# A fused convolution network on one core: spreading the steps of a group-norm statistic over the chunks of layer 1 and computing its shift there

## The chip, the cores and the metric

The kernel runs on 1 core of one Trainium2 chip. The metric is the device time of one execution in microseconds, the median of several runs. Before the change it is 4012.31 us (three runs, 4012.15 to 4015.99).

## The reference

Four layers work on `x` of shape (2, 128, 64, 64), float32. Each normalizes its input in 32 groups of channels, applies its function and adds the result to `x`:

```python
def _gn(v, G=32, eps=1e-5):
    B_, C_, H_, W_ = v.shape
    g = v.reshape(B_, G, C_ // G, H_, W_)
    m = jnp.mean(g, axis=(2, 3, 4), keepdims=True)
    s = jnp.var(g, axis=(2, 3, 4), keepdims=True)
    return ((g - m) / jnp.sqrt(s + eps)).reshape(v.shape)
...
x = x + _L0_conv_ref(_gn(x), ...)
x = x + _L1_conv_ref(_gn(x), ...)
x = x + _L2_conv_ref(_gn(x), ...)
x = x + _L3_conv_ref(_gn(x), ...)
```

Layers 0 and 3 are attention over the 4096 pixels. Layer 1 sums a depthwise 5x5 convolution with dilation 2, a depthwise 1x5 convolution of a 1x3 convolution, and a product with weights that are themselves a correlation of the input. Layer 2 is a product of quaternions in the frequency domain: a 2-D Fourier transform, a product with stored weights at each frequency, and the transform back. The change lies where layer 1 ends and layer 2 begins.

## The kernel before

The activations `X` stay in on-chip memory as a tile of 128 channels by 2 images by 4096 pixels; each layer adds to it in place. A chunk is 512 pixels, so an image has 8 chunks.

**Order.** Layers 1 and 2 open with `_in_order` (L536, L807; the context manager is at L1328): every instruction of TensorE, VectorE, ScalarE and GpSimd is tied to the one before it on its engine as the program writes them. So the order of each of those queues is the order of the Python code, and nothing moves ahead of a waiting instruction of its queue[...]. DMAs are issued from SyncE's queue.

**The statistics.** `_stats_steps` (L1407) is a generator of 11 steps for one image: eight `bn_stats`, one a chunk (L1418); the aggregation `bn_aggr` (L1421); the mean's step, which is a matmul that averages over each group of four channels (L1424), a copy of the mean to the first column of its result (L1429), a difference (L1431) and a square (L1433); and the variance's step, which is a second such matmul (L1436), the addition of epsilon on VectorE (L1403) and the power -0.5 on GpSimd (L1404), both into the second column. So the result is the mean and the reciprocal deviation of each channel. The caller advances it by `next`, and by that decides between which other instructions a step stands.

**The last loop of layer 1** runs over the images `b` and the chunks `c` (L747 to L768). In chunk 0 and 2 of an image, TensorE first computes eight of the 25 + 5 taps of the depthwise convolutions for half an image as small matmuls (`on_tiles`, L681), and ScalarE copies the sums to a tile `z` (L691). In every chunk it computes seven matmuls into one PSUM bank (`combined`, L710). VectorE then adds to `X` the bank of the chunk before (`added`, L721), and after chunks 1, 3 also the half image `z`. After that VectorE works off some of the taps of the depthwise convolution of the second image (`taps`, L662, each over half an image of 2048 pixels: 4, 2, 4, 2, 3, 2, 2, 2 of them in the eight chunks), and then the loop advances the statistics by two steps. There are no statistics to advance for the first image. When it is finished, its remaining additions are made, and `steps` becomes the generator for the first image as layer 2 needs it (into `there`, a slice of the tile `st` of the kernel's main function). So its steps fall into the second image's chunks: two `bn_stats` in each of chunks 0 to 3, the aggregation and the mean's step in chunk 4, the variance's step in chunk 5, and none is left for chunks 6 and 7. After the loop, the last chunk of the second image is added (L721 again).

**The first loop of layer 2** (from L849) runs over the images. VectorE first computes `shift`, minus the mean times the reciprocal deviation (L852). ScalarE normalizes eight columns of the image at a time (`normalized`, L860), and two steps of the second image's statistics follow in VectorE's queue; TensorE transposes them (L870), VectorE copies the result (L876), TensorE multiplies by the Fourier matrix (L883), ScalarE copies the product to `y` (L884). This is skewed over eight such blocks an image. Ahead of it stand three small memsets (L810, L816, L817) and SyncE's loads of the first spectral weights (L823).

The tile `st` in the main function has a slice of two columns for each of the two images of layer 1, for the first image of layer 2 and for that of layer 3.

Of the kernel before, what the change touches and what calls it, by code (L numbers as in the profile page):

```python
# [10 lines left out]
F32 = mybir.dt.float32  # L11
AF = mybir.ActivationFunctionType
ALU = mybir.AluOpType
# [3 lines left out]
B, C, H, W = 2, 128, 64, 64  # L17
# [514 lines left out]
def _layer1(ctx, tc, X, a, cst, here=None, there=None, consts=None):  # L532


    nc = tc.nc
# [183 lines left out]
    def added(b, lo, x):  # L719
        to = X[:, b, lo : lo + x.free_size()]  # L720
        nc.vector.tensor_add(to, x, to)  # L721

    def some(gen, n):
        for _ in range(n):
            next(gen, None)
# [21 lines left out]
    steps = iter(())  # L747
    ready = []
    for b in range(B):
        for c in range(NCH):  # L750
            if c in (0, 2):
                z = on_tiles(g[b], t2[b], c // 2)
            ps = combined(t9[b], t2[b], c)

            for x in ready:
                added(*x)
            ready = [(b, c * CH, ps)]
            if c in (1, 3):
                ready.append((b, c // 2 * S // 2, z))
            some(rest, (4, 2, 4, 2, 3, 2, 2, 2)[c])  # L760
            some(steps, 2)
        if there is not None and b == 0:
            for x in ready:
                added(*x)
            ready = []
            steps = _stats_steps(nc, two, bank, X[:, 0, :], cst, mhalf, there)
    for x in ready:
        added(*x)  # L768

# [33 lines left out]
def _layer2(ctx, tc, X, weights, cst, src, here=None, there=None, beside=None):  # L803


    nc = tc.nc
# [23 lines left out]
    with tc.tile_pool(name="l2_a", reuse_waits="tile", bufs=3) as ap, tc.tile_pool(  # L830
        name="l2_aps", reuse_waits="tile", bufs=4, space=PSUM
    ) as aps:
        def stats(b, st):
            return _stats_steps(
                nc,
                ap,
                lambda: aps.tile([128, CH], F32, tag="pt", name="ps_stat"),
                X[:, b, :],
                cst,
                mhalf,  # L840
                st,
            )

        st = here
        if st is None:
            st = ap.tile([128, 2], F32, tag="st", name="st")
            for _ in stats(0, st):
                pass
        for b in range(B):  # L849
            xw = X[:, b, :].rearrange("p (h w) -> p w h", w=W)  # L850
            shift = ap.tile([128, 1], F32, tag="shift", name="shift")
            nc.vector.scalar_tensor_tensor(shift, st[:, 0:1], -1.0, st[:, 1:2], ALU.mult, ALU.mult)  # L852
            scale = st[:, 1:2]
            if b + 1 < B:
                st = ap.tile([128, 2], F32, tag="st", name="st")
                steps = stats(b + 1, st)

            def normalized(i):
                g = ap.tile([128, 8, H], F32, name="g")
                nc.scalar.activation(  # L860
                    g, xw[:, 8 * i : 8 * i + 8, :], AF.Identity, bias=shift, scale=scale
                )
                for _ in range(2):
                    next(steps, None)
                return g

            def columns(i, g):
                pt = aps.tile([128, CH], F32, tag="pt", name="ps_pt")
                for n in range(4):
                    nc.tensor.transpose(  # L870
                        pt[:, n * 128 : (n + 1) * 128],
                        g[:, 2 * n : 2 * n + 2, :].rearrange("p w h -> p (w h)"),
                        ident,
                    )
                gt = ap.tile([128, CH], F32, name="gt")
                nc.vector.tensor_copy(gt, pt)  # L876
                return gt

            def transformed(i, gt):
                py = aps.tile([128, CH], F32, tag="py", name="ps_py")  # L880
                for n in range(4):
                    cols = slice(n * 128, (n + 1) * 128)
                    nc.tensor.matmul(py[:, cols], gt[:, cols], k["fwd_h"], start=True, stop=True)  # L883
                nc.scalar.copy(  # L884
                    y[:, b, 8 * i : 8 * i + 8, :, :].rearrange("p w c f -> p (w c f)"), py
                )

            gs, gts = {}, {}
            for i in range(W // 8 + 2):
                if i < W // 8:  # L890
                    gs[i] = normalized(i)
                if 1 <= i <= W // 8:
                    gts[i - 1] = columns(i - 1, gs.pop(i - 1))
                if i >= 2:
                    transformed(i - 2, gts.pop(i - 2))

    two = ctx.enter_context(tc.tile_pool(name="l2_two", reuse_waits="tile", bufs=2))
    with tc.tile_pool(name="l2_e", reuse_waits="tile", bufs=4) as ep, tc.tile_pool(
        name="l2_ps", reuse_waits="tile", bufs=2, space=PSUM
# [222 lines left out]
    with tc.tile_pool(name="l2_c", reuse_waits="tile", bufs=3) as cp, tc.tile_pool(  # L1122
        name="l2_cps", reuse_waits="tile", bufs=4, space=PSUM
    ) as cps:
        for b in range(B):
# [25 lines left out]
            steps = iter(())  # L1151
# [255 lines left out]
def _stats_steps(nc, pool, psum_tile, x, cst, mhalf, got, by_scalar=False):  # L1407

    def taken(ps, name):
        if not by_scalar:  # L1410
            return ps[:, 0:1]
        t = pool.tile([128, 1], F32, tag=name, name=name)
        nc.scalar.copy(t, ps[:, 0:1])
        return t

    st = pool.tile([128, NCH, 6], F32, tag="gn_st", name="gn_st")
    for c in range(NCH):
        nc.vector.bn_stats(st[:, c, :], x[:, c * CH : (c + 1) * CH])  # L1418
        yield
    mv = pool.tile([128, 2], F32, tag="gn_mv", name="gn_mv")  # L1420
    nc.vector.bn_aggr(mv, st)  # L1421
    yield
    pm = psum_tile()
    nc.tensor.matmul(pm[:, 0:1], cst["group"], mv[:, 0:1], start=True, stop=True)  # L1424
    mean = got[:, 0:1]
    got_mean = taken(pm, "gn_pm")
    if by_scalar:
        yield
    nc.vector.tensor_copy(mean, got_mean)  # L1429
    d = pool.tile([128, 1], F32, tag="gn_d", name="gn_d")  # L1430
    nc.vector.tensor_sub(d, mv[:, 0:1], mean)  # L1431
    e = pool.tile([128, 1], F32, tag="gn_e", name="gn_e")
    nc.vector.scalar_tensor_tensor(e, d, d, mv[:, 1:2], ALU.mult, ALU.add)  # L1433
    yield
    pv = psum_tile()
    nc.tensor.matmul(pv[:, 0:1], cst["group"], e, start=True, stop=True)  # L1436
    var = taken(pv, "gn_pv")
    if by_scalar:
        yield
    _power(nc, pool, got[:, 1:2], var, 0.0, 1e-5, mhalf)  # L1440
    yield
# [1058 lines left out]
@with_exitstack  # L2500
def kernel(ctx, tc, a, out):
    nc = tc.nc
    flagp = ctx.enter_context(tc.tile_pool(name="flag", bufs=1))
    within = flagp.tile([1, 1], mybir.dt.int32, name="within")
    dram = ctx.enter_context(tc.tile_pool(name="dram", bufs=1, space=bass.MemoryType.DRAM))
    with tc.tile_pool(name="keep", bufs=1) as keep:
        X, cst, eps5 = _inputs(tc, keep, a)

        worst = keep.tile([128, 1 + 2 * B], F32, name="worst")
        st = keep.tile([128, B + 2, 2], F32, name="st")  # L2510
        rows_of_weights = _layer0(tc, X, a, cst, worst, st[:, :B], dram)
        with tc.tile_pool(name="late", reuse_waits="tile", bufs=1) as late:
            with tc.tile_pool(name="raw", reuse_waits="tile", bufs=1) as raw:
                with tc.tile_pool(name="l1_in", reuse_waits="tile", bufs=1) as l1_in:
                    consts = _layer1_inputs(nc, l1_in, a)
                    l3 = _layer3_inputs(nc, late, raw, a, a["consts2"])
                    _layer1(tc, X, a, cst, st[:, :B], st[:, B], consts)
                _layer2(
                    tc,
                    X,  # L2520
                    rows_of_weights,
                    cst,
                    a["consts1"],
                    st[:, B],
                    st[:, B + 1],
                    lambda: _layer3_weights(nc, l3),
                )
            _layer3(tc, X, l3, cst, out, worst, st[:, B + 1], dram)
        with tc.tile_pool(name="flag_ps", reuse_waits="tile", bufs=1, space=PSUM) as fp:
            most = keep.tile([128, 1], F32, name="most")  # L2530
            nc.vector.tensor_reduce(most, worst, AX.X, ALU.max)
            pt = fp.tile([1, 128], F32, name="ps_most")
            nc.tensor.transpose(pt, most, cst["ident"])
            top = keep.tile([1, 1], F32, name="top")
            nc.vector.tensor_reduce(top, pt, AX.X, ALU.max)
            nc.vector.tensor_scalar(within, top, LIMIT, None, ALU.is_le)

    ok = nc.values_load(within[0:1, 0:1])
    with tc.If(ok == 0):
        _general(tc, a, out)  # L2540
# [57 lines left out]
```

## Time and profile before

| | |
|---|---|
| median of three runs | 4012.31 us |
| lowest and highest | 4012.15, 4015.99 us |
| the profiled execution's own time | 4012.48 us |
| its span in the profile | 4010.7 us |
| mean granted clock of TensorE | 0.985 |
| taps on VectorE (L662), 84 | 2.351 us each |
| aggregation (L1421), in this stage | 0.37 us |
| power on GpSimd (L1404), in this stage | 0.56 us |
| normalization of one block (L860), layer 2 | 1.28 us |

The profile is taken on one execution. It has a page with the busy time of the engines and the chain of work that ended last, and its trace can be asked for groups of instructions by line, for the waits (who waited for whom), for the chain in order of time, for the instructions of an engine in a stretch of time, and for busy time and clock in such stretches. PE is TensorE's matmuls, PEld its weight loads, DVE VectorE, ACT ScalarE, POOL GpSimd, SP SyncE. L12 is line 12 of the kernel. Times within it are microseconds from the start of the span. A name left of `<-` is what an instruction writes, those right of it what it reads. The ends of matmuls are modelled.

### The profile page before, as it was taken

What the parts mean: (1) busy time and instruction counts of PE and PEld (TensorE: products, weight loads), DVE (VectorE), ACT (ScalarE), POOL (GpSimd) and SP (SyncE); (2) the same over time, 40 slices, a digit from 0 to 9 for tenths busy, and PEclk for the clock granted to TensorE, in tenths of its full rate; (3) what the DMA queues carried; (4) which work ended last, traced back from release to release, by engine and by line L of the source; (5) the groups of instructions that cost most, each with busy time, mean ns of one, the idle gap of its engine ahead of it and who ended that gap; (6) DMA issues with size and microseconds to landing.
All of it is one profiled execution on the core that took longest, in us unless ns stands there. A gap on an engine that the chain in (4) does not pass through costs nothing.

```text
span 4010.7 us, 82168 instructions
## 1 busy us (share of the span) xinstructions
PE 3857.8 (96%) x35214; PEld 1318.5 (33%) x35214; DVE 3197.1 (80%) x3572; ACT 3247.0 (81%) x3955; POOL 86.2 (2%) x145
## 2 busy tenths in 40 slices
PE   7999999989999998997998999999999999999998
PEld 4511222353111124445664332232223222322222
DVE  6599999858999998995758777777777777776666
ACT  4499999736899983226645999999999999999998
POOL 1000000000000001000000000000000000000000
PEclk9999999999999999998999999999999999999999
DMA  1199960000000000004654100110002000110000
GB/s 51 24 201 189 187 98 2 1 2 2 2 2 2 2 1 13 6 38 176 268 215 149 33 31 26 53 46 30 27 25 74 30 27 25 43 48 6 6 6 4
DMA packets 193128, 217.59 MB, mean 54 GB/s; under 512 B 30441, under 2 KB 154345, under 8 KB 188658
## 3 DMA queue, kind: packets, MB, share of 16 engines
q1 hardware_dynamic: 192754, 212.25, 20.4%
q8 instruction: 278, 4.55, 0.5%
q14 instruction: 96, 0.79, 0.1%
HBM read 178.64 MB, written 98.57 MB: 69 GB/s over the span
## 4 chain that ended last, share of the span: by engine, by line
PE 81%; DVE 7%; issue 4%; ACT 3%; POOL 0%; DMA 0%; SPq 0%; POOLq 0%; ACTq 0%; DVEq 0%
PE ps_acc L2313 25%; PE ps_s L2290 19%; PE ps L1858 11%; PE ps L1866 11%; PE ps_bank L710 2%; PE ps_z L1008 2%; DVE sums L1889 2%; PE ps L1619 2%; DVE e L950 1%; PE ps_t L640 1%; PE ps_bank L590 1%; PE ps_bank L1062 1%; PE ps_bank L681 1%; PE ps_acc L2171 1%; PE ps_acc L2217 1%
## 5 line engine op out<-in xcount | busy, mean ns | idle before, releaser
L2304 ACT ACTIVATE weights<-ps_s 128x1024 f32<-128x1024 f32 x1920 | 1781.4, 1063 | 76.4 <-PE ps_s L2290 76.2
L2313 PE MATMUL ps_acc<-weights,vt 128*32 128x512 f32 x8192 | 1092.9, 605 | 0.0
L1889 DVE TENSOR_TENSOR sums<-sums,weights 128x2048 f32<-128x2048 f32 x384 | 854.2, 2283 | 3.5 <-ACT weights L1941 1.2
L2290 PE MATMUL ps_s<-q,k 64*128 64x512 f32 x4096 | 830.6, 469 | 4.3 <-DMA k<-stack 2.8
L1941 ACT ACTIVATE weights<-ps 128x1536 f32<-128x1536 f32 x512 | 740.6, 1446 | 6.9 <-PE ps L1866 6.9
L2290 PEld LDWEIGHTS ps_s<-q,k 64*128 64x128 f32 x4096 | 348.4, 184 | 936.6 <-ACT weights L2304 809.4
L1866 PE MATMUL ps<-q,k 32*64 32x512 f32 x8192 | 574.0, 612 | 3.6 <-ACT weights L1938 3.0
L1858 PE MATMUL ps<-weights,vt 128*32 128x512 f32 x4096 | 544.6, 604 | 0.0
L2262 DVE SCALAR_TENSOR_TENSOR exp_z<-exp_z,exp_m 128x1024 f32<-128x1024 f32 x384 | 468.9, 1221 | 9.3
L1938 ACT ACTIVATE weights<-ps 128x512 f32<-128x512 f32 x512 | 306.8, 599 | 75.4 <-PE ps L1866 36.5
L2246 DVE TENSOR_SCALAR exp_i<-ps_s 128x1024 int32<-128x1024 f32 x128 | 156.7, 1224 | 216.4 <-PE ps_s L2290 216.2
L2313 PEld LDWEIGHTS ps_acc<-weights,vt 128*32 128x32 f32 x8192 | 161.9, 108 | 309.3 <-issue 308.5
L1866 PEld LDWEIGHTS ps<-q,k 32*64 32x64 f32 x8192 | 120.0, 129 | 432.1 <-ACT weights L1938 381.6
L1858 PEld LDWEIGHTS ps<-weights,vt 128*32 128x32 f32 x4096 | 84.3, 108 | 390.9 <-issue 378.5
L662 DVE SCALAR_TENSOR_TENSOR X<-g,w,X 128x2048 f32<-128x2048 f32 x84 | 197.4, 2351 | 2.6
L2266 DVE SCALAR_TENSOR_TENSOR weights<-exp_z,exp_i 128x1024 f32<-128x1024 f32 x128 | 156.8, 1225 | 15.9 <-ACT weights L2304 0.5
L1889 DVE TENSOR_TENSOR sums<-weights 128x2048 f32<-128x2048 f32 x64 | 145.7, 2288 | 28.7 <-ACT weights L1941 27.9
L1619 PE MATMUL ps<-pad,diag 32*32 32x512 f32 x4032 | 151.8, 614 | 8.7 <-DVE qk L1630 4.1
L2262 DVE SCALAR_TENSOR_TENSOR exp_z<-exp_m 128x1024 f32<-128x1024 f32 x128 | 155.9, 1218 | 0.0
L1008 PE MATMUL ps_z<-w_ri,e 128*32 128x128 f32 x2048 | 137.5, 409 | 14.6 <-DVE e L950 12.4
L1619 PEld LDWEIGHTS ps<-pad,diag 32*32 32x32 f32 x4032 | 86.2, 104 | 69.2 <-issue 21.1
L950 DVE TENSOR_SCALAR e<-ps_pe 32x136 f32<-32x136 f32 (+1 forms) x352 | 104.4, 297 | 5.0
(314 smaller groups left out, 2953.5 us busy)
## 6 DMA issues: line engine op xcount, KB each, us to landing
w_ri<-w_r SPq DMA_DIRECT2D x16, 2112.0 KB, 7.9
w_ri<-w_i SPq DMA_DIRECT2D x16, 2112.0 KB, 13.7
stack<-qs SPq DMA_DIRECT2D x64, 256.0 KB, 2.1
q<-stack SPq DMA_DIRECT2D x128, 128.0 KB, 2.5
k<-stack SPq DMA_DIRECT2D x128, 128.0 KB, 2.5
stack<-ks SPq DMA_DIRECT2D x32, 256.0 KB, 2.1
w_r<-in_L_conv_kr_w SPq DMA_DIRECT2D x15, 528.0 KB, 12.3
w_r<-in_L_conv_kr_x SPq DMA_DIRECT2D x15, 528.0 KB, 12.5
```

The costliest lines, as they stand in the source:

```text
L662: nc.vector.scalar_tensor_tensor(xi, g[:, i : i + H // 2, j : j + W], w8[:, s : s + 1], xi, ALU.mult, ALU.add)
L1008: nc.tensor.matmul(out.rearrange("p (n f o) -> p n f o", n=2, f=2), e[:, s, 2 * j : 2 * j + 2, :].rearrange("p f x -> p (f x)"), w.rearran ...
L1619: nc.tensor.matmul(ps[r // 2][to, r % 2, :].rearrange("p (h w) -> p h w", w=W), diag[rows, grp, t, :], pad[rows, y0 : y0 + ROWS, t % 3 : t ...
L1858: nc.tensor.matmul(out[rows, :], lhs(rows), w[:, j, :], start=first, stop=stop)
L1866: nc.tensor.matmul(bank[64 * h : 64 * h + 64, :], k1[rows, kt * 128 + 64 * h : kt * 128 + 64 * h + 64], q1[rows, qb * CH : (qb + 1) * CH], ...
L1889: nc.vector.tensor_add(parts[p].rearrange("p j c -> p (j c)"), t.rearrange("p j c -> p (j c)"), w.rearrange("p j c -> p (j c)"),)
L1938: nc.scalar.activation(held[n][:, 0, :], single, AF.Exp)
L1941: nc.scalar.activation(held[n][:, 1:, :], three, AF.Exp)
L2262: nc.vector.scalar_tensor_tensor(z, x, n, m, ALU.add, ALU.mult)
L2290: nc.tensor.matmul(ps[j // 2][:, j % 2, :], g.k[kt // 4][rows, j // 2, keys], g.q[qb][rows, j // 2, :], start=True, stop=True,)
L2304: nc.scalar.activation(w[0], ps[p], AF.Exp)
L2313: nc.tensor.matmul(g.ac[32 * j : 32 * j + 32, :], g.vt[:, kt, j // 2, i : i + 2, :].rearrange("p a d -> p (a d)"), w[:, i, :], start=(at = ...
```

## The change

In the last loop of layer 1, the number of steps that a chunk advances the statistics by is now a table: 2, 2, 2, 2, 1, 1, 1, 0. It holds for both images; for the first there are still no steps. After the loop, ahead of the last chunk's addition, `shift` is computed in layer 1 into a third column of `there`. Layer 2 uses that column for its first image where it is given, and computes the shift as before otherwise. The tile `st` gets three columns a slice in place of two.

```diff
@@ in _layer1, the last loop
             some(rest, (4, 2, 4, 2, 3, 2, 2, 2)[c])
-            some(steps, 2)
+            some(steps, (2, 2, 2, 2, 1, 1, 1, 0)[c])
         if there is not None and b == 0:
             for x in ready:
                 added(*x)
             ready = []
             steps = _stats_steps(nc, two, bank, X[:, 0, :], cst, mhalf, there)
+    if there is not None:
+        nc.vector.scalar_tensor_tensor(
+            there[:, 2:3], there[:, 0:1], -1.0, there[:, 1:2], ALU.mult, ALU.mult
+        )
     for x in ready:
         added(*x)
@@ in _layer2
         for b in range(B):
             xw = X[:, b, :].rearrange("p (h w) -> p w h", w=W)
-            shift = ap.tile([128, 1], F32, tag="shift", name="shift")
-            nc.vector.scalar_tensor_tensor(shift, st[:, 0:1], -1.0, st[:, 1:2], ALU.mult, ALU.mult)
+            if b == 0 and here is not None:
+                shift = here[:, 2:3]
+            else:
+                shift = ap.tile([128, 1], F32, tag="shift", name="shift")
+                nc.vector.scalar_tensor_tensor(
+                    shift, st[:, 0:1], -1.0, st[:, 1:2], ALU.mult, ALU.mult
+                )
             scale = st[:, 1:2]
@@ in tile_conv_preact_kernel
-        st = keep.tile([128, B + 2, 2], F32, name="st")
+        st = keep.tile([128, B + 2, 3], F32, name="st")
```

## The prediction

> **What bounds the kernel now.** I read the page's first and fourth parts for the whole, then only the stage that the change touches: the last 30 us of layer 1 and the first 10 us of layer 2 (about 1762 to 1805 us of the span), first by its waits, then VectorE in order of time, then the chain, then TensorE's clock.
>
> ```profile
> PE 3857.8 (96%) x35214; PEld 1318.5 (33%) x35214; DVE 3197.1 (80%) x3572; ACT 3247.0 (81%) x3955; POOL 86.2 (2%) x145
> PE 81%; DVE 7%; issue 4%; ACT 3%; POOL 0%; DMA 0%; SPq 0%; POOLq 0%; ACTq 0%; DVEq 0%
> ```
>
> TensorE carries 81% of the chain over the whole span. That average says nothing of this stage, so the waits of 1768 to 1796 us come next (who waited, for whom: us in total, times, longest).
>
> ```profile
> PE ps_bank L1424 <- DVE gn_mv L1421: 4.9, 1, 4.9
> DVE st L1403 <- PE ps_bank L1436: 2.4, 1, 2.4
> DVE X L721 <- PE ps_bank L710: 1.3, 2, 0.7
> DVE st L1429 <- PE ps_bank L1424: 0.7, 1, 0.7
> ```
>
> TensorE and VectorE take turns in waiting for each other. VectorE in order of time (start, duration, in brackets the idle time before it and its releaser) shows it:
>
> ```profile
> 1772.85 0.37 DVE L1421 BATCH_NORM_AGGREGATE gn_mv<-gn_st 128x2 f32<-128x48 f32 x1
> 1773.95 0.16 DVE L1429 COPY st<-ps_bank 128x1 f32<-128x1 f32 x1 [0.74 <-PE ps_bank L1424]
> ...
> 1774.47 0.68 DVE L721 TENSOR_TENSOR X<-ps_bank,X 128x512 f32<-128x512 f32 x1
> 1775.19 4.74 DVE L662 SCALAR_TENSOR_TENSOR X<-g,w,X 128x2048 f32<-128x2048 f32 x2
> 1782.33 0.16 DVE L1403 TENSOR_SCALAR st<-ps_bank 128x1 f32<-128x1 f32 x1 [2.39 <-PE ps_bank L1436]
> ...
> 1788.52 0.69 DVE L721 TENSOR_TENSOR X<-ps_bank,X 128x512 f32<-128x512 f32 x1 [0.66 <-PE ps_bank L710]
> 1789.24 4.74 DVE L662 SCALAR_TENSOR_TENSOR X<-g,w,X 128x2048 f32<-128x2048 f32 x2
> 1794.60 0.69 DVE L721 TENSOR_TENSOR X<-ps_bank,X 128x512 f32<-128x512 f32 x1 [0.62 <-PE ps_bank L710]
> 1795.37 0.15 DVE L852 SCALAR_TENSOR_TENSOR shift<-st 128x1 f32<-128x1 f32 x1
> ```
>
> The mean's product (L1424) stands in TensorE's order ahead of chunk 5's seven products, and cannot run before VectorE's aggregation ends at 1773.22. TensorE had finished chunk 4 at about 1768.5, so chunk 5 waits 4.9 us for work it doesn't need. From then on VectorE waits for TensorE: 0.74 + 2.39 + 0.66 + 0.62 = 4.41 us. The chain (start, us, what) tells the same:
>
> ```profile
> 1772.93 0.29 DVE gn_mv L1421
> 1773.22 0.14 issue
> 1773.36 0.56 PE ps_bank L1424 x2
> 1773.91 8.26 PE ps_bank L710 x14
> ```
>
> Chunk 5's matmuls take 8.26 us here; the next 28 take 12.3, so 14 should take 6.2. The windows (stretch, us, busy of PE, PEld, DVE, ACT, POOL, then clock) say why:
>
> ```profile
> 1768.50:1773.30 4.80, 0.00 (x0) 0.00 (x0) 4.68 (x3) 0.00 (x0) 0.00 (x0) 0.78 0.00 0
> 1773.30:1778.20 4.90, 4.84 (x8) 2.37 (x9) 4.11 (x6) 0.00 (x0) 0.00 (x0) 0.52 0.01 3
> 1798.50:1802.00 3.50, 3.50 (x18) 3.46 (x17) 3.45 (x6) 1.99 (x3) 0.00 (x0) 0.51 0.99 422
> ```
>
> The pause costs TensorE its clock: half speed until about 1778, some 2.1 us more. A second half-speed stretch follows layer 1's end.
>
> [...] clock 1.00 until 1771.0, 0.54 and 0.52 to 1778.2, then 1.00. [...] the addition at 1774.47 had its bank complete since 1768.5 and stood behind the copy at L1429. [...] the trace has 0.69 us for 512 elements and 2.29 for 2048[...], so a one-column operation is nearly all fixed cost, as the 0.15 to 0.16 us rows here show.
>
> **The change, part by part.** I use durations and start-to-start distances of the same rows: an addition followed by a tap that waits for it 0.72 us, two taps 4.74.
>
> *Steps one a chunk.* The counts per chunk become 2, 2, 2, 2, 1, 1, 1, 0 in place of 2 throughout. For the first image there are no steps, so only the second image's chunks 4 to 7 change: aggregation stays in chunk 4, the mean's step goes to chunk 5, the variance's to chunk 6. Nothing is added or removed; the built order agrees: L1424 now follows chunk 5's products, L1436 chunk 6's, the copy, difference and square (L1429 to L1433) follow chunk 5's taps, L1403 chunk 6's.
>
> TensorE then: chunk 4 ends 1768.45; chunk 5 waits only for copies of `z` that ended at 1759.5 and for old matmuls, so it runs 1768.5 to 1774.6 (6.1 us, at full clock, no pause); L1424 (aggregation ready 1773.22, so no wait) to 1774.9; chunk 6 to 1781.0; L1436; chunk 7 1781.2 to 1787.3.
>
> VectorE: aggregation from 1772.85; addition of chunk 4 at 1773.25, taps 1773.97 to 1778.7; L1429, L1431, L1433 (their product has been done 3.8 us) from 1778.65 at 0.19 each; addition of chunk 5 at 1779.2 (its products ended at 1774.6); taps 1779.9 to 1784.6; L1403 at 1784.55 (L1436 has been done since about 1781.1); addition of chunk 6 at 1784.7; taps 1785.4 to 1790.2. No wait is left: the least margin is the last addition's, 1790.3 against 1787.3. GpSimd's power (0.56 us) runs at about 1785.0 to 1785.6.
>
> *Shift ahead of the last additions.* It is one operation of 0.15 us, moved from after layer 2's memsets (1795.37) to before the last addition. It waits for GpSimd's power, over for 4.5 us; queued behind it are the last addition, the memsets and the next image's statistics. It runs at about 1790.1 to 1790.25. ScalarE's first normalization (L860) waited for the shift; it now starts at about 1790.3 in place of 1795.55, **5.25 us** earlier. The last addition ends at about 1790.95 in place of 1795.29, 4.34 earlier: the 4.41 of stalls less a few hundredths.
>
> *What reaches the end.* The extra 0.9 us of ScalarE is not all worth it: VectorE's copy of the first transposes (L876) stands behind the last addition, two memsets and four statistics. Before, it came 3.22 us after the last addition's start (1794.60 to 1797.82); now about 3.17: 1793.43, **4.39 us** earlier. The first transposes are ready before that (1790.3 + 1.3 + 1.06 at half clock = 1792.7). So layer 2's first products start 4.4 us earlier, and everything after is in the same order.
>
> *Clock at the seam.* TensorE now pauses 4.3 us (1787.3 to 1791.6) in place of 2.3. [...] Before, half clock lay from 1798.5 to 1801.9, which in the new times is 1794.1 to 1797.5: squarely on the first products. At best those 2.08 us become 1.06 and ScalarE's waits of 1.51 and 0.24 us there shrink, a gain of up to 1.3[...]. I take **0.3** of gain.
>
> *Other edits.* `st` grows from 32 to 48 bytes a partition; the tiles after it move by 32 bytes. VectorE's rows for tiles at both offsets lie on one line ((2283-1221)/1024 = 1.037 ns an element, (1221-690)/512 = 1.037), so I take 0, with 1 us either way in the range. SyncE's order is the same; its first weight loads of layer 2 wait for chunk 7's products and the last tap, so they go out at about 1790.3 in place of 1794.70. They are wanted at 1837; the slowest such load took 22.5 us, so this is covered by some 18 us. The second transposes now wait for VectorE and TensorE counts that are over 3 us old: 0.
>
> **Sum.** 4.4 + 0.3 = 4.7 us. Against the profiled execution: span 4010.7 - 4.7 = 4006.0, and 1.8 around it (4012.48 - 4010.7) gives 4007.8. Its 4012.48 is 0.17 over the median of 4012.31, so the median forecast is **4007.6 us**, 0.12% less. A measurement of this kernel can tell about 0.2% from no change, 8.0 us, so by that bound this is the same.
>
> **Rivals.**
> 1. *Stalls go, but the clock takes back part*: half clock spans one window more on layer 2's first blocks. Price 2 us in place of the 0.3: 4012.3 - 4.4 + 2 = 4009.9. For it: the pause is now longer. Against: from 1794.2 on the products come densely enough to fill a window, as they did from 1798.5 before.
> 2. *Absorbed later*: a later stage is released by something that doesn't move, and the time is 4012.3. Against: DMA has 0% of the chain, SyncE's first loads move too, and no queue I find in layer 2 starts by anything older.
> 3. *The other side, slower*: the longer pause leaves TensorE at half clock through the whole first image of layer 2's first stage[...]. A block then takes 1.06 + 2.08 = 3.14 us on TensorE against ScalarE's pace of 1.7: 1.44 more for each of six further blocks, 8.6, so 4012.3 - 4.4 + 8.6 = 4016.5. It decides from three such blocks on (4.4 / 1.44), some 9 us of half clock. Against: before, one window cured it (1.00 from 1802 on) with the same bursts.
> 4. *More than forecast*: the half clock falls off both images' products; ScalarE's waits there (1.51 + 0.24, and 1.39 + 0.28 for the second image) go: 4012.3 - 4.4 - 3.4 = 4004.5.
>
> **Chances.** Forecast 0.72, with 4005.8 to 4009.2 as its own range; rival 1 0.11, rival 2 0.05, rival 3 0.04, rival 4 0.08. About half of rival 4 lies beyond 0.2% (under 4004.3), and I add 0.01 for what isn't foreseen: faster 0.05. Slower by over 0.2% (over 4020.3) needs rival 3 with still more of it, or the moved addresses to cost: 0.02. Within 0.2%: 0.93. The three runs before spread over 3.8 us, so the range is 4004.6 to 4011.5: it takes in rival 1 and nearly all of the forecast.
>
> **What would show it.** Right: no wait of L1424 for the aggregation and none of VectorE in the last four chunks, chunk 5's products in 6.1 us at clock 1.00, the shift about 0.2 us ahead of the last addition, and ScalarE's first L860 at about 1790.3. The first L876 should stand at about 1793.4, and the weight loads at about 1790.3. Wrong: a VectorE wait for `ps_bank` beyond 1775, TensorE's clock at 0.5 beyond 1798, or the same distance from the seam to the end being longer than before by more than 2 us.

## The result and the profile after

| | before | changed |
|---|---|---|
| median | 4014.48 us | 4005.72 us |
| lowest and highest of 20 runs | 4008.67, 4018.25 | 4003.59, 4012.53 |
| the profiled execution's own time | 4012.48 | 4004.01 |
| its span | 4010.7 | 4002.2 |

The ratio is 0.9981, with a 95% interval of [0.9974, 0.9987]. (It is the comparison's own estimate; the quotient of the two medians is 0.9978.) The forecast was 4007.6 us, which is 0.9988 of its base; the measured median lies 1.9 us below it and inside the range. The ratio asks for some 7.6 us where the forecast had 4.7, so the question for the rest of this document is whether the seam between the layers gave what it should, and where the other 3 us are from.

All views below are of the changed kernel. Its lines are shifted: the statistics are nine lines further on (aggregation L1430, the two products L1433 and L1445, the copy of the mean L1438, epsilon L1412), and so is layer 2 (normalization L869, transposes L879, their copy L885, products L892, copy to `y` L893). The shift is L768. From the page, the busy times and the chain:

```profile
PE 3852.0 (96%) x35214; PEld 1315.7 (33%) x35214; DVE 3197.0 (80%) x3572; ACT 3247.1 (81%) x3955; POOL 86.1 (2%) x145
PE 50%; DVE 3%; issue 0%; ACT 0%; DMA 0%; SPq 0%; POOL 0%; DVEq 0%; ACTq 0%
```

VectorE and ScalarE work as long as before, to 0.1 us: no work was removed. TensorE's busy time is 5.8 us less with the same number of matmuls. The trace's record of the clock has 120.1 us at half clock over the span in place of 123.2, which by my estimate (half of 3.1) accounts for at most some 1.6 us of it; I did not follow the rest. The chain's shares sum to 53% here: it couldn't be followed back as far as the seam, and I read nothing from it. The waits of 1760 to 1796 us, who waited for whom (us in total, times, longest):

```profile
...
PE ps_pt L879 <- ACT g L869: 4.5, 1, 4.5
ACT y L893 <- PE ps_py L892: 2.4, 1, 2.4
...
PE ps_py L892 <- DVE gt L885: 0.3, 1, 0.3
DVE X L721 <- DVE gn_mv L1430: 0.2, 1, 0.2
```

Neither a wait of a statistics product for the aggregation nor one of VectorE for a bank is left. What remains of VectorE's is 0.2 us for its own aggregation. TensorE now has one pause of 4.5 us behind the last product, where before it had 4.9 us ahead of chunk 5's and 2.3 behind the last. VectorE in order of time (start, duration, in brackets the idle time before it and its releaser):

```profile
1771.22 0.37 DVE L1430 BATCH_NORM_AGGREGATE gn_mv<-gn_st 128x2 f32<-128x48 f32 x1
...
1777.17 0.15 DVE L1438 COPY st<-ps_bank 128x1 f32<-128x1 f32 x1
...
1783.06 0.15 DVE L1412 TENSOR_SCALAR st<-ps_bank 128x1 f32<-128x1 f32 x1
1783.17 0.69 DVE L721 TENSOR_TENSOR X<-ps_bank,X 128x512 f32<-128x512 f32 x1
1783.90 4.74 DVE L662 SCALAR_TENSOR_TENSOR X<-g,w,X 128x2048 f32<-128x2048 f32 x2
1788.56 0.15 DVE L768 SCALAR_TENSOR_TENSOR st<-st 128x1 f32<-128x1 f32 x1
1788.74 0.69 DVE L721 TENSOR_TENSOR X<-ps_bank,X 128x512 f32<-128x512 f32 x1
...
1790.12 1.86 DVE L1427 BATCH_NORM_STATS2 gn_st<-X 128x6 f32<-128x512 f32 x3
1791.89 0.68 DVE L885 COPY gt<-ps_pt 128x512 f32<-128x512 f32 x1
```

The queue is full from the aggregation to the first copy of transposes. TensorE in the same stretch (durations of a row are from the first start to the last end):

```profile
1754.56 18.40 PE L710 MATMUL ps_bank<-t,t 128*128 128x512 f32 x42
1772.80 0.28 PE L1433 MATMUL ps_bank<-gn_mv,consts 128*128 128x1 f32 x2
1772.93 6.33 PE L710 MATMUL ps_bank<-t,t 128*128 128x512 f32 x14
1779.10 0.28 PE L1445 MATMUL ps_bank<-gn_e,consts 128*128 128x1 f32 x2
1779.24 6.33 PE L710 MATMUL ps_bank<-t,t 128*128 128x512 f32 x14
1790.07 2.30 PE L879 MATMUL ps_pt<-consts,g 128*128 128x128 f32 x8 [4.50 <-ACT g L869]
1792.62 2.08 PE L892 MATMUL ps_py<-consts,gt 128*128 128x128 f32 x8 [0.26 <-DVE gt L885]
```

The first row is chunks 3 to 5 without a gap: 6.13 us a chunk, where chunk 5 took 8.26. Each statistics product runs as soon as the chunk ahead of it is done. But the first transposes and Fourier products of layer 2 ran at half clock. Four transposes took 1.06 us from 1794.49 on and 0.66 from 1798.83 on, at full clock; the eight matmuls of the last row took 2.08 us, as the first eight did before, where eight took 1.06 from 1797.43 on. The windows (stretch, us, busy of PE, PEld, DVE, ACT, POOL, then clock) put bounds on that:

```profile
1771.00:1785.50 14.50, 14.50 (x37) 6.27 (x35) 14.06 (x14) 0.00 (x0) 0.56 (x1) 1.00 0.00 1
1785.50:1790.00 4.50, 0.07 (x1) 0.00 (x0) 4.37 (x8) 1.26 (x2) 0.00 (x0) 0.97 0.23 49
1790.00:1794.50 4.50, 4.11 (x17) 3.31 (x18) 4.50 (x9) 2.36 (x3) 0.00 (x0) 0.50 0.85 340
1794.50:1797.00 2.50, 2.50 (x16) 2.50 (x16) 2.01 (x4) 1.77 (x2) 0.00 (x0) 0.59 1.01 433
1797.00:1805.00 8.00, 7.36 (x61) 6.71 (x62) 3.78 (x9) 7.39 (x9) 0.55 (x1) 1.00 1.01 433
```

Half clock lies from about 1789.7 (the 0.97 of the second row) to 1796.5 (2.05 us of the fourth), 6.8 us, where before it was 3.4 at this place, and another 6.8 at chunk 5, which are gone. One more stretch of 3.4 us, between the two images of layer 2, is in both (1815.6 to 1819.0 before, 1810.2 to 1813.6 now).

Absolute times of two executions don't compare: the last loop of layer 1 starts at 1653.92 us before and at 1652.29 in the changed kernel, though nothing ahead of it differs but the addresses. So I count from the first product of that loop (L681). The aggregation then starts at 118.93 in both. The columns are starts in us: first normalization, last addition, first copy of transposes, first and eighth copy to `y` (the end of the first image), and VectorE's first copy in the spectral stage that follows both images.

| | norm. | addition | copy | `y` 1st | `y` 8th | spectral |
|---|---|---|---|---|---|---|
| before | 141.64 | 140.68 | 143.90 | 146.74 | 158.29 | 177.99 |
| changed | 136.45 | 136.46 | 139.60 | 142.45 | 154.24 | 173.94 |
| gain | 5.19 | 4.22 | 4.30 | 4.29 | 4.05 | 4.05 |

The seam gives 4.05 us, which is 0.9990. The profiled pair differs by 8.5: 1.63 ahead of the loop, 4.05 here, and 2.8 after the spectral stage begins.

### The profile page after: what moved, and what is told of

It is laid out like the page before. It is cut to its first block, busy times and chain, and to the rows that moved or that the text cites. A ratio compares the mean times of both kernels' runs of the same rounds, so it can differ in the third digit from the quotient of the medians.

```text
span 4002.2 us, 82168 instructions
## 1 busy us (share of the span) xinstructions
PE 3852.0 (96%) x35214; PEld 1315.7 (33%) x35214; DVE 3197.0 (80%) x3572; ACT 3247.1 (81%) x3955; POOL 86.1 (2%) x145
## 4 chain that ended last, share of the span: by engine, by line
PE 50%; DVE 3%; issue 0%; ACT 0%; DMA 0%; SPq 0%; POOL 0%; DVEq 0%; ACTq 0%
PE ps_acc L2322 25%; PE ps_s L2299 19%; PE ps_z L1017 2%; DVE e L959 1%; PE ps_bank L1071 1%; PE ps_acc L2180 1%; PE ps_acc L2226 1%; PE ps_pe L934 1%; DVE z L1026 0%; PE ps_bank L921 0%; DVE exp_z L2271 0%; PE ps_bank L1046 0%; PE ps_po L1156 0%; DVE top L2206 0%; DVE gn_st L1427 0%
## 5 line engine op out<-in xcount | busy, mean ns | idle before, releaser
L1017 PE MATMUL ps_z<-w_ri,e 128*32 128x128 f32 x2048 | 137.4, 409 | 14.5 <-DVE e L959 12.1
```

The lines of the kernel that those rows point to most:

```text
L1017: nc.tensor.matmul(out.rearrange("p (n f o) -> p n f o", n=2, f=2), e[:, s, 2 * j : 2 * j + 2, :].rearrange("p f x -> p (f x)"), w.rearran ...
```

## The experiments

The leading theory: the gain is chunk 5's release from the aggregation, by the table alone, and is over at the seam. Rivals: it is the early shift; it is the spreading as such; the moved tiles bring something outside the seam; or the clock decides how much reaches the end.

**The halves and the width.** The kernel before with the table alone, so with the shift in layer 2 and two columns:

```diff
-            some(steps, 2)
+            some(steps, (2, 2, 2, 2, 1, 1, 1, 0)[c])
```

> The kernel before with the table of steps (2, 2, 2, 2, 1, 1, 1, 0) alone; the shift stays in layer 2, and no tile moves. My theory (the stalls between VectorE and TensorE at the end of layer 1 are the gain): VectorE's four waits (4.41 us) go, the first copy of layer 2's transposes comes 4.3 us earlier as counted from the aggregation, ScalarE's first normalization also 4.3; time 4.3 to 4.7 us less, ratio 0.9988 to 0.9989. Rival, the moved addresses: the same distances at the seam, but the part of the gain beyond 4.7 us (ratio 0.9981 for the whole change) is missing because nothing moves. Rival, the shift: if the early shift carries the gain, the time is that of before.

Measured: 0.9992 [0.9983, 1.0]. By the trace the first copy of transposes stands at 139.88 and the spectral stage at 174.06, 4.02 and 3.93 us earlier than before. The first normalization is 4.23 us earlier in place of 5.19. So the table carries the seam, and the early shift adds 0.12 us at its end. The interval reaches 1.0; it is the distances in the trace that tell this run from the kernel before.

The shift alone, which is the changed kernel with two steps in every chunk:

```diff
-            some(steps, (2, 2, 2, 2, 1, 1, 1, 0)[c])
+            some(steps, 2)
```

> The change without its table: two steps a chunk as before, the shift computed in layer 1 ahead of the last addition, the tile of statistics 16 bytes wider. My theory: ScalarE's first normalization starts 1.6 us earlier (1794.0 for 1795.55), but the first copy of the transposes stands behind the last addition, which still waits for TensorE, so it gains 0.1 us; ratio 1.0000. Rival, the moved addresses: 3 us less, ratio 0.9993. Rival, the shift: most of the gain, ratio 0.9985 or less.

Measured: 1.0 [0.9992, 1.0009]. Its waits of 1768 to 1797 us keep the old pause:

```profile
...
PE ps_bank L1433 <- DVE gn_mv L1430: 4.9, 1, 4.9
DVE st L1412 <- PE ps_bank L1445: 3.0, 1, 3.0
```

VectorE waited 3.0 us for the variance's product in place of 2.4, since more of the half clock lay on chunk 5's products (9.06 us from the first start to the last end, in place of 8.40). The window just behind the pause has the clock at half throughout:

```profile
1773.50:1779.00 5.50, 5.38 (x8) 2.61 (x9) 4.65 (x6) 0.00 (x0) 0.00 (x0) 0.50 0.01 3
```

The last addition came 0.67 us later than before, the normalization 0.80 us earlier, and the first copy at 144.50 against 143.90. The early shift frees ScalarE sooner, but the copy stands behind the last addition and the statistics in VectorE's queue, so nothing of it arrives there. The spectral stage still began at 177.32, 0.67 us earlier than before: this execution has no half clock between the two images, which the run on the clock below puts at 1.22 us.

The third column alone, in the kernel before:

```diff
-        st = keep.tile([128, B + 2, 2], F32, name="st")
+        st = keep.tile([128, B + 2, 3], F32, name="st")
```

> The kernel before with the tile of statistics widened from two to three columns and nothing else: all tiles allocated after it move by 32 bytes a partition, no instruction changes. My theory: no effect, ratio 1.0000, the first 60 us of layer 0 included. Rival, the moved addresses: about 3 us less, ratio 0.9993, of it some 2.9 us in the first 40 us of layer 0, where the profile of the changed kernel is ahead by that much.

Measured: 1.0003 [0.9995, 1.0011]. The spectral stage begins at 177.83. Moving the tiles by 32 bytes does nothing that shows.

The whole change with the shift in a spare column of another tile (`worst`, four bytes longer), and `st` with its two columns:

```diff
-            there[:, 2:3], there[:, 0:1], -1.0, there[:, 1:2], ALU.mult, ALU.mult
+            moved, there[:, 0:1], -1.0, there[:, 1:2], ALU.mult, ALU.mult
...
-        worst = keep.tile([128, 1 + 2 * B], F32, name="worst")
+        worst = keep.tile([128, 2 + 2 * B], F32, name="worst")
```

> The whole change, but the shift goes to a spare column of another small tile, so that the tiles stay where they were before. My theory: the full gain, 4.7 us, ratio 0.9988, and the same as the changed kernel's if its further 3 us are scatter. Rival, the moved addresses: 4.7 us while the changed kernel has 7.6, so the time is 3 us above the changed kernel's.

Measured: 0.9988 [0.9981, 0.9994], with the spectral stage at 173.90. The gain stays when the column goes; the column is not its cause.

**Spread, but with the variance's step in chunk 5.** If spreading as such were the cause, the mean's and the variance's step could share a chunk that doesn't follow the aggregation:

```diff
-            some(steps, (2, 2, 2, 2, 1, 1, 1, 0)[c])
+            some(steps, (2, 2, 2, 2, 1, 2, 0, 0)[c])
```

> The changed kernel with the table (2, 2, 2, 2, 1, 2, 0, 0): the mean's and the variance's step both in chunk 5. So the variance's product stands right behind the mean's on TensorE and waits for VectorE's square behind chunk 5's taps. The steps are still spread over one chunk more than before, and the shift is early. My theory (what counts is which products stand behind a wait): TensorE pauses for 4.7 us after the mean's product, then runs at half clock for some 5 us; VectorE waits about 3 us for chunk 6's bank; the last addition comes 21.1 us after the aggregation, against 17.5 in the changed kernel and 21.75 before; ratio 0.9998. Rival (spreading alone is the gain): 17.5 us and a ratio of 0.9988.

Measured: 1.0 [0.9991, 1.0008]. Its waits of 1768 to 1797 us:

```profile
...
PE ps_bank L1445 <- DVE gn_e L1442: 4.8, 1, 4.8
DVE X L721 <- PE ps_bank L710: 2.6, 2, 2.0
...
DVE st L1412 <- PE ps_bank L1445: 0.7, 1, 0.7
```

And TensorE in order of time:

```profile
1774.47 0.28 PE L1433 MATMUL ps_bank<-gn_mv,consts 128*128 128x1 f32 x2
1779.58 0.56 PE L1445 MATMUL ps_bank<-gn_e,consts 128*128 128x1 f32 x2 [4.84 <-DVE gn_e L1442]
1780.00 13.79 PE L710 MATMUL ps_bank<-t,t 128*128 128x512 f32 x28
```

The mean's product now waits for nothing, but the variance's needs the square, which stands behind chunk 5's taps in VectorE's queue. So chunk 6 waits 4.8 us in place of chunk 5. The pause has moved by one chunk and kept its length. VectorE's waits for TensorE sum to 3.3 us, and the last addition is 0.84 us earlier than before, not 4.22. The seam ended 2.29 us early: 0.91 are there at the first copy of transposes, and most of the rest comes from full clock behind it, 1.22 us of it between the two images. The ratio shows nothing of this; its interval takes in the 0.9994 that 2.29 us would be. So the rule of the change is not one step a chunk: a product that depends on VectorE must stand so late on TensorE that its input is there.

**The clock at the seam.** Four products of 512 columns that nothing uses, behind chunk 7's, keep TensorE busy into its pause:

```diff
+    if there is not None:
+        spare = bank()
+        for _ in range(4):
+            nc.tensor.matmul(spare, ident, t9[1][:, 0:4, :].rearrange("p k c -> p (k c)"), start=True, stop=True)
     for x in ready:
         added(*x)
```

> The changed kernel with four matmuls of 512 columns added on TensorE behind chunk 7's products; their result is used by nothing. They fill 3.5 us of the pause of 4.5 us between layer 1 and layer 2. My theory (the clock at the seam is worth little): the first copies of the transposes come no earlier, since they stand behind VectorE's statistics; TensorE is at full clock for layer 2's first products, so up to 1.3 us less from there to layer 2's first spread copy, which was 34.3 us after the first copy of the transposes: 33.0 to 34.3. Rival 3 (half clock at the seam eats the gain): 3 us or more less. Rival, the fill itself delays layer 2: 0.5 us or more longer.

Measured: 0.9987 [0.9981, 0.9994]. The windows of the stretch where the changed kernel had half clock, the clock standing after POOL:

```profile
1787.00:1791.00 4.00, 3.81 (x9) 1.32 (x7) 3.93 (x4) 0.45 (x1) 0.00 (x0) 1.00 0.00 0
1791.00:1794.50 3.50, 1.39 (x9) 0.92 (x9) 3.44 (x10) 3.15 (x3) 0.00 (x0) 1.00 0.85 285
1794.50:1797.00 2.50, 2.31 (x19) 2.08 (x20) 2.50 (x5) 1.38 (x2) 0.00 (x0) 1.00 1.01 429
```

The clock stays at 1.00. The first copy of transposes is where it was (139.57 against 139.60): VectorE's queue sets it, not the clock. The first copy to `y` comes 0.96 us earlier, the eighth 0.44, and the spectral stage begins at 172.28 in place of 173.94. The 1.66 us have two parts. At the end of the first image 0.44 us are left of what full clock at the seam saved. The other 1.22 come behind it, since this execution has no half clock between the two images either: from the eighth copy to `y` to the spectral stage it takes 18.48 us, and so do the other three executions without that stretch (the variance's step in chunk 5, the shift alone, the copy first: 18.47 to 18.48), while the ten that have it take 19.67 to 19.75. The ratio (0.9987 beside 0.9988 of the run with unmoved tiles) shows nothing of this.

**The copy first, then an earlier shift.** The 0.97 us by which ScalarE is ahead of the last addition's gain might be had if the copy of transposes did not stand behind four statistics. Layer 2's two statistics steps per block go behind the copy:

```diff
             def normalized(i):
...
-                for _ in range(2):
-                    next(steps, None)
...
                     gts[i - 1] = columns(i - 1, gs.pop(i - 1))
+                    for _ in range(2):
+                        next(steps, None)
```

> The changed kernel with layer 2's own steps of the second image's statistics put behind the copy of a block's transposes instead of ahead of it, so that four of them no longer stand ahead of the first copy. My theory (VectorE's queue holds the first copy back, not ScalarE): the first copy waits for the transposes alone and starts 20.0 us after the aggregation in place of 20.67; everything behind gains 0.7 us; ratio 0.9986. Rival (ScalarE's start sets layer 2): no gain.

Measured: 0.9985 [0.9978, 0.9992]. The copy is at 138.91, 0.69 us earlier than in the changed kernel, and now waits 1.63 us for the transposes. The spectral stage begins at 173.27, 0.67 us earlier, which looks like the forecast gain but is not: the eighth copy to `y` is 0.56 us later than in the changed kernel (154.80), and what makes up for it is the missing half clock between the images, 1.22 us. Within the first image TensorE's product of the second image's mean (L1433) now waits 1.32 us for its aggregation, which it didn't in the changed kernel.

With that, the statistics begin with three steps in chunks 0 and 1, and the shift is taken after chunk 6's taps:

```diff
-            some(steps, (2, 2, 2, 2, 1, 1, 1, 0)[c])
+            some(steps, (3, 3, 2, 1, 1, 1, 0, 0)[c])
+            if there is not None and (b, c) == (1, 6):
+                nc.vector.scalar_tensor_tensor(
+                    there[:, 2:3], there[:, 0:1], -1.0, there[:, 1:2], ALU.mult, ALU.mult
+                )
...
-    if there is not None:
-        nc.vector.scalar_tensor_tensor(
-            there[:, 2:3], there[:, 0:1], -1.0, there[:, 1:2], ALU.mult, ALU.mult
-        )
```

> The same as the run with the copies first, and the statistics of layer 1 finished earlier too: table (3, 3, 2, 1, 1, 1, 0, 0), and the shift after chunk 6's taps. So ScalarE can normalize three blocks, and TensorE transpose them, while VectorE still works on the last chunks. My theory: ScalarE starts at least 5 us ahead of the last addition, the first copy follows directly on the last addition (2.5 us earlier than in the changed kernel), and with ScalarE three blocks ahead the whole gain is 2.5 to 4.5 us over the changed kernel; ratio to before 0.9978 to 0.9983. Rival (VectorE's own work per block then binds layer 2's first image): 2.5 us at most and the rest given back within the image.

Measured: 0.9981 [0.9973, 0.9989]. The normalization starts at 130.07, 6.38 us earlier than in the changed kernel, and the copy follows the last addition at once:

```profile
1782.64 0.15 DVE L763 SCALAR_TENSOR_TENSOR st<-st 128x1 f32<-128x1 f32 x1
...
1788.40 0.69 DVE L721 TENSOR_TENSOR X<-ps_bank,X 128x512 f32<-128x512 f32 x1
...
1789.17 0.69 DVE L883 COPY gt<-ps_pt 128x512 f32<-128x512 f32 x1
```

The first copy to `y` is 3.41 us earlier than in the changed kernel, but the eighth only 1.81, and the spectral stage 1.84 (172.10). So half of the new lead is gone by the end of the first image. The trace speaks against VectorE's own work as the cause, since its copies wait for transposes there, 3.3 us in four waits. The product of the second image's mean waits for its aggregation on TensorE here too (1.15 us), and the next copy to `y` behind it waits 1.63; whether that is the whole of it was not tested.

The same with two unused products between the first transposes and the first Fourier products, to keep the clock up:

```diff
+                if b == 0 and i == 2 and here is not None:
+                    spare = aps.tile([128, CH], F32, tag="py", name="ps_py")
+                    for _ in range(2):
+                        nc.tensor.matmul(spare, ident, X[:, 0, 0:CH], start=True, stop=True)
```

> The kernel with the early shift and the copies first, and two matmuls of 512 columns added on TensorE between the first two blocks' transposes and the first products of layer 2, their result used by nothing. There TensorE paused 3.0 us. My theory (half clock behind that pause costs up to 1 us): the first product ends 0.8 us earlier and layer 2's first spread copy 0.5 to 1.5 us earlier, at 170.6 to 171.6 us from the same starting point; ratio 0.9978 to 0.9981. Rival (the filling delays the first product): 0.5 us later.

Measured: 0.9984 [0.9976, 0.9991]. The clock was 1.00 from 1787 to 1801 us and the first copy to `y` another 0.66 us earlier, but the spectral stage began at 173.28, 1.18 us later than without them. What they saved at the start was more than lost. The trace shows where: from the first to the eighth copy to `y` it takes 15.15 us in place of 13.39. A stretch of half clock now lies inside the first image (145.9 to 149.3 us), and the product of the second image's mean waits 2.05 us in place of 1.15; which of the two weighs more was not tested. Neither of these versions is told from the changed kernel by its time.

**Repeats.** The changed kernel, and in a later comparison the kernel before and the table alone, each unaltered:

> The changed kernel once more, unaltered, to see what of its gain is scatter. The stretch from layer 1's last part to layer 2's first spread copy was 4.05 us shorter in its profile, and the same instructions at the old addresses gave 0.9988. My theory (the seam is worth 4 to 4.7 us and the rest is scatter of the stretches that are equal in both): ratio 0.9985 to 0.9991, and the same 173.9 us from the first small matmul of the last image half's pair to the first spread copy. Rival (something else in the change gives 3 us more): 0.9981 again.

Measured: 0.9985 [0.9978, 0.9992], 4005.07 against 4011.99 us. The copy is at 139.61 and the spectral stage begins at 173.57, 4.42 us earlier than before. Half clock lasted 6.8 us as in the first execution, but began 135.7 us from the loop's start in place of 137.4, so that more of it lay in the pause.

> The kernel before, unchanged. It shows how far a comparison of two identical kernels strays. If what the two comparisons of the changed kernel gave beyond the seam (0.9981 and 0.9985 against 0.9990 from 4.05 us) is scatter of such comparisons, this one can stray by as much: 0.9995 to 1.0005. If it lies within 0.0002 of 1, the two are harder to put down to scatter, and a gain outside the seam is likelier.

Measured: 1.0001 [0.9992, 1.0009]. The medians of these two identical kernels are 4011.33 and 4013.25 us, 1.9 apart. Its seam ends at 177.87.

> The table of steps alone once more, the shift in layer 2. Its seam ends 0.12 us later than that of the whole change (first spread copy 174.06 against 173.94 us after the last loop's start). Theory that the seam is all: 0.9990, and equal to the whole change within the interval. Rival, a gain that goes with the early shift or with the third column: 0.9990 to 0.9992 here again while the whole change has 0.9981 to 0.9985. Rival, a gain beyond the seam that goes with the table: 0.9983 here too.

Measured: 0.9988 [0.9981, 0.9995], where the first comparison of the same kernel had 0.9992. Its seam ends at 174.09.

## Why the prediction was right, and where it was off

**The stalls: right.** The forecast had VectorE's four waits gone, 4.41 us, and the last addition 4.34 us earlier; it came 4.22 earlier. The signs that it named for this are there: no wait of the mean's product for the aggregation, none of VectorE for a bank, and chunk 5's products in 6.13 us at clock 1.00 (forecast 6.1). The shift stands 0.18 us ahead of the last addition (forecast 0.2). The run with the variance's step moved back to chunk 5 brings the pause back one chunk later, at 4.84 us.

**The early shift: right in place and in worth.** Forecast 5.25 us at the first normalization, measured 5.19; forecast 4.39 at the copy, measured 4.30, because the copy stands behind the last addition and four statistics. The shift alone gave no time (1.0), the table alone 4.02 of those 4.30 us.

**The clock: the mis-sized term.** The 0.3 us of gain that the forecast took was its author's estimate. The pause was forecast at 4.3 us and measured at 4.50. Half clock lasted from 137.4 to 144.3 us from the loop's start, which is 1791.4 to 1798.2 of the forecast's times, just past the 1798 that it had named as a sign of being wrong. So it lasted 6.83 us at this place in place of 3.41, one window more, as rival 1 has it. In the clock records of these two executions each stretch of one clock, but the last of each record, is a whole multiple of 3.413 us long, and two stretches of half clock in the changed kernel start at 1789.73 and 1810.21 us, which is six times 3.413 apart. A pause of 2.3 us was followed by half clock before. Windows of 3.41 us that begin or end at a change of the clock show how much TensorE worked in each: three of the changed kernel, then two of the kernel before at the seam, then three of the run with the variance's step in chunk 5:

```profile
1786.31:1789.73 3.42, 0.00 (x0) 0.00 (x0) 3.33 (x7) 0.99 (x1) 0.00 (x0) 1.00 0.00 0
1789.73:1793.14 3.41, 2.75 (x10) 1.95 (x11) 3.41 (x7) 2.63 (x3) 0.00 (x0) 0.50 1.02 339
1793.14:1796.56 3.42, 3.42 (x18) 3.42 (x17) 3.37 (x7) 1.77 (x2) 0.00 (x0) 0.50 1.00 425
...
1795.08:1798.49 3.41, 1.12 (x8) 0.84 (x8) 3.35 (x11) 2.94 (x3) 0.00 (x0) 1.00 0.86 282
1798.49:1801.91 3.42, 3.42 (x18) 3.37 (x16) 3.37 (x7) 1.91 (x3) 0.00 (x0) 0.50 0.98 417
...
1772.60:1776.02 3.42, 2.15 (x7) 0.94 (x5) 3.19 (x4) 0.00 (x0) 0.00 (x0) 1.00 0.01 2
1776.02:1779.43 3.41, 0.00 (x0) 0.00 (x0) 3.30 (x5) 0.00 (x0) 0.00 (x0) 1.00 0.00 0
1779.43:1782.84 3.41, 3.26 (x6) 1.74 (x7) 2.63 (x4) 0.00 (x0) 0.56 (x1) 0.50 0.00 0
```

A window that TensorE's matmuls filled by a third (1.12 of 3.41 us) was followed by half clock, one that they filled by 0.63 (2.15) was not; and at half clock one filled by 0.81 (2.75) was followed by half clock again, where one filled by 0.96 (3.26) was followed by full clock. What the forecast sized wrong was the return: it counted on products dense enough to fill a window, and the first window of half clock was filled by 0.81.

Rival 1 priced the extra window at a loss of 2 us. It cost far less, since most of it fell ahead of the first copy of transposes, on the pause and on transposes that VectorE's queue reached later anyway: the gain at the copy is 4.30. From the copy on, half clock at the seam lasted 3.4 us before, 4.7 in the first execution (1791.89 to 1796.56) and 2.9 in the repeat, where the windows lay 1.8 us earlier. With that goes the sign: from the copy to the spectral stage 0.25 us of the gain were lost in the first, and 0.13 added in the repeat (4.29 to 4.42). So in these two executions the term is worth -0.25 to +0.13 us, by where the windows lay. With TensorE kept busy the gain rises to 5.71 (177.99 - 172.28), 1.22 of it by the stretch between the images. Rival 3, half clock through the whole image, didn't occur: the clock was 1.00 from 1797 to the image's end. Rival 2, a gain absorbed later, didn't either: 4.05 us are still there where the spectral stage begins, and no comparison of the changed kernel came out at 1. Rival 4, no half clock on either image, is met in two other runs, that with unused products and that with the variance's step in chunk 5. From the first copy of transposes to the spectral stage both take 32.71 us, 1.4 less than the 34.09 of before, where rival 4 had 3.4.

**The addresses and the weight loads: nothing, as taken.** The third column alone gave 1.0003 [0.9995, 1.0011]. SyncE's first weight load went out at 1788.80 us, which is 136.51 from the loop's start against 140.78 before, with the rest of the seam.

**The sum.** 4.7 us was forecast for the seam, 4.05 and 4.42 measured in two executions, against one of the kernel before; its repeat and the run with the third column alone end the seam at 177.87 and 177.83 in place of 177.99, so some 0.2 us of these figures is scatter. The comparisons give 0.9981 and 0.9985 for the changed kernel, 0.9988 for the same with unmoved tiles, 0.9992 and 0.9988 for the table alone; in the profiles of these five, the spectral stage begins between 173.57 and 174.09. The mean of the five ratios is 0.9987. Each interval but the first includes the forecast's 0.9988, and the first ends at 0.9987. So the 3 us beyond the forecast in the first comparison may in part be scatter: one kernel gave 0.9992 and 0.9988. But the kernel before against itself gave 1.0001, within the 0.0002 that had been named as speaking for a gain outside the seam, though with an interval of 0.0008 on either side this decides little. In the profiles, the stretch ahead of the loop takes from 1652.0 to 1657.5 us and the one behind the spectral stage from 2174.9 to 2184.7, whichever kernel it is, and both ends of the latter are of kernels that have the gain.

This scatter goes with the clock: over the 14 profiles, the stretch behind the spectral stage lengthens with the half clock in it, from 69 us of it at 2174.9 to 100 at 2184.7 (correlation 0.92); and of 193 executions of the kernel before in the later comparisons, the 25 with a mean clock of 0.982 have a median of 4019.45 us, the 81 with 0.985 one of 4010.90. At 0.985 alone the changed kernel, in its two comparisons, has a median of 4004.55 us in 17 executions, 6.35 less, so the clock's scatter, as far as its three listed digits show it, doesn't explain the remainder away. **What stays open** is whether some 1 or 2 us of the remainder belong to the change. The intervals are 0.07% wide on either side, about 2.8 us, and don't settle it. Nor do they settle whether the early shift brings more than its 0.12 us: the table alone averages 0.9990, the three with the shift 0.9985, less apart than the width of one interval.

The forecast that a measurement would call this the same by 0.2% held for the ratio (0.9981 is 0.19%), though its interval excludes 1.

## What to carry to other kernels

In a queue that runs in order, as TensorE's does in this stage, a tiny product that waits for another engine holds back the independent products behind it (4.9 us ahead of chunk 5 here), so read the wait's own row and then ask what stands behind it; place such a product after the work that covers its input's delay, and check each dependent product by itself, since freeing the first can move the same pause to the second (4.8 us ahead of chunk 6). A result that is ready earlier is worth only as much as the slowest queue between it and the end: 5.19 us at ScalarE were 4.30 at VectorE's next copy. For changes of 0.1%, read the gain from distances between fixed marks in the trace and repeat the comparison, since equal stretches of two executions here differ by more than the change is worth. Compare the clock along these distances too: one stretch of half clock more or less, 1.22 us here, can pass for a gain, as it did in the run with the copy first.

## What the runs showed of the hardware

- In these traces the share of a window of 3.413 us that TensorE's matmuls filled goes with the clock of the next, the windows being laid off from a change of the clock. Of the 45 windows that begin from 100 to 178 us after the loop's start in the profiled executions of the kernel before and of the changed kernel, 38 are at full clock: the six filled by 0.00 to 0.41 were followed by half clock, the 32 filled by 0.65 or more by full clock. Seven are at half clock: the two filled by 0.36 and 0.81 were followed by half clock, the five that were filled throughout by full clock. This is read off the traces; no run varied the share alone.
- So the pause's length alone doesn't decide. After 4.50 us of pause at the seam half clock lasted 6.83 us in the changed kernel; 4.84 us ahead of chunk 6, with the variance's step in chunk 5, were followed by 3.41, and the window behind it was filled by 0.96. With TensorE busy for 3.6 us of the pause by the unused products, the clock was 1.00 in each stretch read from 1787 to 1815 us.
- The clock's loss after one and the same pause varies. With the order of before, the half clock at chunk 5 lasted 6.8 us in each of four executions (the kernel before, its repeat, the third column alone and the shift alone), but chunk 5's products took 8.40 us in the first and 9.06 in the last: the pause of 4.86 us was the same in these two, and how much of the half clock fell into it wasn't.
